# A convolution-mixer layer with a mixture of experts on one core: the gate's products on parts of the array, and other spacing of three stages

## The chip, the cores and the metric

The kernel runs on one core of one Trainium2 chip. The time is that of the device for one execution, in microseconds (us), from the first to the last instruction of the core; the number of a kernel is the median of its runs. Everything is in 32-bit floats. A core has these engines: PE (TensorE, matrix products; PEld is its loading of weights), DVE (VectorE), ACT (ScalarE, functions from tables and the eviction of PSUM), POOL (GpSimd), and SP, which here only issues DMAs. Each takes its instructions in the order in which the program has them.

## The reference, cut to what matters

For each of 4 images of 256 channels x 1024 positions:

```python
xs = x.reshape(B, C, N).transpose(0, 2, 1)            # after a norm over channels
xn = layernorm(xs, norm_w, norm_b)
xm = mamba_v(xc, ...) + skip_scale * xc               # 4 blocks of 64 channels, a selective scan over N
Q  = conv1d(conv1d(x_concat, qdw_w, qdw_b, groups=NB, pad=1), qpw_w, qpw_b)   # NB = 4 outputs, then 4x4
g  = sigmoid(Q);  xg = g * xm                         # one gate for each block of 64 channels
R  = conv1d(conv1d(xgt, rdw_w, rdw_b, groups=C, pad=1), rpw_w, rpw_b) + xgt
cat = concatenate([xs, R]);  xm2 = conv1d(conv1d(cat, fdw_w, fdw_b, groups=2*C, pad=1), fpw_w, fpw_b) + xs
x_local = conv1d(xm2, lc_w, lc_b, groups=C, pad=1);  x_global = mha(xm2, ...)  # 8 heads of 32
x_out = gelu(layernorm(concatenate([x_local, x_global]) @ fc_w.T + fc_b))
# norm over positions, 3x3 depthwise convolution, layernorm, product with proj_w, residual
# then for every position: norm, top 2 of 8 experts (256 -> 1024 -> gelu -> 256), weighted sum, residual
```

The change concerns `Q` and `g`, the end of the convolutions (`fpw_w`), the first norm of a next image, and the norms of the last image.

## The kernel before

The program is written in beats. In the main loop a beat is one step of the scan of the image at hand (32 states x 4 rows by 512 positions): the step's own instructions, and then one turn of each running generator, such as the convolutions of the image before. `yield n` in a generator means that it goes on n beats later. So the text decides where an instruction stands in its engine's queue; no scheduler moves it. Image b has 8 parts of 16 steps. The convolutions of image b-1 run in the first four parts of image b, its attention right after part 3, without scan steps beside it but the next ones. For the last image there is no scan left; its stages run beside tiles of the experts, each of 256 rows (64 products for a tile).

```python
def step(b, n, h, i):                                       # the scan
    dBu = ps(...)                                           # a PSUM tile
    nc.vector.tensor_tensor(dBu, dts[:, 1, :], bs, ALU.mult)
    nc.vector.tensor_tensor_scan(hs, dA, dBu, 0.0 if h == 0 else last, ALU.mult, ALU.add)
    if h == 0:
        nc.gpsimd.tensor_copy(last, hs[:, HALF - 1 : HALF])
    nc.gpsimd.tensor_tensor(hs, hs, cs, ALU.mult)
# bs: four products of PE on 32 columns each; dA: ACT; u: projection of the next block ("up", 4 products a half)

def in_turn(items, make, use, lag=2):
    made = []
    for at in range(len(items) + lag):
        if at >= lag:
            use(items[at - lag], made[at - lag])
        if at < len(items):
            made.append(make(items[at]))
        yield 1

def convolutions(b):
    ...                                                     # depthwise taps of xl, on ACT and DVE
    while not T.get(("whole", b)):
        yield 1
    xm = XM.pop(b)
    qs, qd = [], []
    for h in range(2):
        qd.append(ps(f"qd_{b}_{h}"))
        for i in range(6):
            c, k = divmod(i, 3)
            nc.tensor.matmul(qd[h][0:NB], qdwT_s[:, c, k, :], xm[:, c, ds(k + h * HALF, HALF)],
                             start=(i == 0), stop=(i == 5))
            if i % 3 == 2:
                yield 1
    for h in range(2):
        yield 1 - h
        qs.append(a2(f"qs_{b}_{h}", NB))
        nc.scalar.activation(qs[h], qd[h][0:NB], AF.Identity, bias=col("qdw_b", 0, slice(0, NB)))
    yield 1
    def gate(c): ...            # gp[h] = product of qpwT_s[:, ts(c, P)] (4 rows) and qs[h], both halves
    def sigmoid(c, gp): ...     # ACT, and back to the table of exp and ln
    yield from in_turn(range(NC2), gate, sigmoid)
    ...                         # POOL: xm = g * xm; taps of xm; rp = product with rpwT_s; residual on DVE; taps d4r
    yield from in_turn(CO_H, <fp: 4 products with fpwT_s into one PSUM tile>, mixed)   # mixed: DVE adds fp to xl
    yield from prepared(b)      # values (vp), queries and keys (qkp) of the attention

def normalised(b):              # first norm of an image to come
    ...
    for c in range(NC2):
        xl = a4(f"xl_{b}_{c}")
        nc.gpsimd.tensor_tensor(xl, xn[:, c, LEFT:], r1, ALU.mult)
        yield 1
        nc.vector.tensor_tensor(xn[:, c, LEFT:], xn[:, c, LEFT:], r2, ALU.mult)   # after POOL has read xn
        ...

def inverse_deviation(name, xc, alone):                     # alone: the last image
    ...
    for h in range(2):
        yield 1
        var.append(column_mean(f"var_{name}_{h}", sq[h]))
    for h in range(2):
        yield 1
        root(r[:, half(h)], var[h], eps5)                   # ACT: ln, then exp
    for c in range(NC2):
        nc.vector.tensor_tensor(xc[:, c, :], xc[:, c, :], r, ALU.mult)
        yield 1
```

Of the kernel before, what the change touches and what calls it, by code (L numbers as in the profile page):

```python
# [9 lines left out]
F32 = mybir.dt.float32  # L10
# [4 lines left out]
P = 128  # L15
# [57 lines left out]
def network(  # L73
# [70 lines left out]
    with tc.tile_pool(name="w_conv", bufs=1) as wp, tc.tile_pool(  # L144
# [33 lines left out]
        aoutT_s = load(aoutT, "aoutT_s")  # L178
        projT_s = load(projT, "projT_s")
        fcT_s = load(fcT, "fcT_s")  # L180
        qdwT_s = load(qdwT, "qdwT_s")
        qpwT_s = load(qpwT, "qpwT_s")
        rpwT_s = load(rpwT, "rpwT_s")
        fpwT_s = load(fpwT, "fpwT_s")
        wvT_s = load(wvT, "wvT_s")
# [9 lines left out]
        def later_weights():  # L195

            nc.sync.dma_start(vb, vbias.rearrange("a (c p) -> p (a c)", p=P))
            for t, ap in later:
                nc.sync.dma_start(t, ap)
                yield 1  # L200
            for ci in range(NC2):
                nc.sync.dma_start(
                    wqkT_s[:, ci].rearrange("p w (i x) -> p (w i) x", x=2 * HD)
                    .rearrange("p c (i x) -> p c i x", x=HD),
                    wqkT[:, ci].rearrange("p c (i x) -> p c i x", x=2 * HD)[:, :, :, 0:HD],
                )
                yield 1
            for i in range(4):
                at = _AT["qk_b"] + i // 2
                nc.sync.dma_start(  # L210
                    qk_b[ts(i, HD), :], vecs[ds(64 * (i % 2), HD), at : at + 8 : 2]
                )
                yield 1

            obp = ps_tile("obp")
            for co in range(NC2):
                for ci in range(NC2):
                    nc.tensor.matmul(
                        obp[:, co : co + 1], aoutT_s[:, ci, ts(co, P)], vb[:, ci : ci + 1],
                        start=(ci == 0), stop=(ci == NC2 - 1),  # L220
                    )
            yield 1
            nc.vector.tensor_tensor(
                ob, obp[:, 0:NC2], V[:, _AT["attn_outb"] : _AT["attn_outb"] + NC2], ALU.add
            )

            prp = ps_tile("prp")
            for co in range(NC2):
                for ci in range(NC2):
                    nc.tensor.matmul(  # L230
                        prp[:, co : co + 1], projT_s[:, ci, ts(co, P)], col("norm_b", ci),
                        start=(ci == 0), stop=(ci == NC2 - 1),
                    )
            yield 1
            nc.vector.tensor_tensor(
                prb, prp[:, 0:NC2], V[:, _AT["proj_b"] : _AT["proj_b"] + NC2], ALU.add
            )
            for ci in range(NC2):
                nc.vector.tensor_scalar(
                    projT_s[:, ci, :], projT_s[:, ci, :], col("norm_w", ci), None, ALU.mult  # L240
                )
            yield 1

            nc.vector.tensor_reduce(fcm, fcT_s, AX.X, ALU.add)
            yield 1
            nc.vector.tensor_scalar(fcm, fcm, 1.0 / C, None, ALU.mult)
            nc.vector.tensor_tensor(
                fcT_s, fcT_s, fcm.to_broadcast([P, 2 * NC2, C]), ALU.subtract
            )
            fbp = ps_tile("fbp")  # L250
            for c in range(NC2):
                nc.tensor.matmul(
                    fbp[:, 0:1], ones_mean, col("fc_b", c), start=(c == 0), stop=(c == NC2 - 1)
                )
            yield 1
            nc.vector.tensor_tensor(
                fcb, V[:, _AT["fc_b"] : _AT["fc_b"] + NC2], fbp[:, 0:1].to_broadcast([P, NC2]),
                ALU.subtract,
            )
# [113 lines left out]
                )  # L373
            return out

        def in_turn(items, make, use, lag=2):

            made = []
            for at in range(len(items) + lag):
                if at >= lag:  # L380
                    use(items[at - lag], made[at - lag])
                if at < len(items):
                    made.append(make(items[at]))
                yield 1

        CO_H = [(co, h) for co in range(NC2) for h in range(2)]

# [52 lines left out]
        def normalised(b):  # L440


            place_xn(b)
            xn = XN[b]

            def part(c, h):
                return xn[:, c, ds(LEFT + h * HALF, HALF)]

            yield 4

            def centre(h, mean):
                for c in range(NC2):
                    nc.vector.tensor_tensor(part(c, h), part(c, h), mean, ALU.subtract)

            yield from in_turn(
                range(2), lambda h: column_mean(f"mean_{b}_{h}", [part(c, h) for c in range(NC2)]),
                centre,
            )
            r1, r2 = a4(f"r1_{b}"), a4(f"r2_{b}")
            for h in range(2):  # L460
                sq = [a2(f"sq_{b}_{h}_{c}") for c in range(NC2)]
                for c in range(NC2):
                    nc.gpsimd.tensor_tensor(sq[c], part(c, h), part(c, h), ALU.mult)
                yield 1
                var = column_mean(f"var_{b}_{h}", sq)
                yield 2
                root(r1[:, half(h)], var, eps6)
                yield 1
                root(r2[:, half(h)], var, eps11, scale=1.0 + 1e-5)
                yield 1  # L470
            for c in range(NC2):
                xl = a4(f"xl_{b}_{c}")
                nc.gpsimd.tensor_tensor(xl, xn[:, c, LEFT:], r1, ALU.mult)
                yield 1
                nc.vector.tensor_tensor(xn[:, c, LEFT:], xn[:, c, LEFT:], r2, ALU.mult)
                yield 1
                nc.sync.dma_start(XL[b][:, c, :], xl)
                nc.gpsimd.tensor_scalar(
                    xn[:, c, LEFT:], xn[:, c, LEFT:], col("norm_w", c), col("norm_b", c),
                    ALU.mult, ALU.add,  # L480
                )
                yield 1
# [258 lines left out]
        def convolutions(b):  # L741
# [8 lines left out]
                yield 1  # L750
            xm = XM.pop(b)

            qs, qd = [], []
            for h in range(2):
                qd.append(ps(f"qd_{b}_{h}"))
                for i in range(6):
                    c, k = divmod(i, 3)
                    nc.tensor.matmul(
                        qd[h][0:NB], qdwT_s[:, c, k, :], xm[:, c, ds(k + h * HALF, HALF)],
                        start=(i == 0), stop=(i == 5),  # L760
                    )
                    if i % 3 == 2:
                        yield 1
            for h in range(2):
                yield 1 - h
                qs.append(a2(f"qs_{b}_{h}", NB))
                nc.scalar.activation(
                    qs[h], qd[h][0:NB], AF.Identity, bias=col("qdw_b", 0, slice(0, NB))
                )
            yield 1  # L770
            def gate(c):
                gp = []
                for h in range(2):
                    gp.append(ps(f"gp_{b}_{c}_{h}"))
                    nc.tensor.matmul(
                        gp[h], qpwT_s[:, ts(c, P)], qs[h], start=True, stop=True
                    )
                return gp

# [35 lines left out]
            def mixed(at, r):  # L815
# [5 lines left out]
                CO_H, lambda at: product(  # L821
                    f"fp_{b}_{at[0]}_{at[1]}", fpwT_s, at[0],
                    [d[ci // 2][:, ci % 2, half(at[1])] for ci in range(4)],
                ), mixed,
            )
            yield from prepared(b)

# [172 lines left out]
        def inverse_deviation(name, xc, alone):  # L1000

            r = a4(f"r_{name}")

            def squares(h):
                sq = [a2(f"sq_{name}_{h}_{c}") for c in range(NC2)]
                for c in range(NC2):
                    nc.scalar.activation(sq[c], xc[:, c, half(h)], AF.Square)
                return sq

            if alone:  # L1010
                sq = [squares(h) for h in range(2)]
                var = []
                for h in range(2):
                    yield 1
                    var.append(column_mean(f"var_{name}_{h}", sq[h]))
                for h in range(2):
                    yield 1
                    root(r[:, half(h)], var[h], eps5)
            else:
                for h in range(2):  # L1020
                    sq = squares(h)
                    yield 1
                    var = column_mean(f"var_{name}_{h}", sq)
                    yield 2
                    root(r[:, half(h)], var, eps5)
# [5 lines that stand above are left out]
# [998 lines left out]
```

## Time and profile before

| | |
|---|---|
| time, median of 3 runs | 2474.78 us (2465.03 to 2476.65) |
| span of the profiled execution | 2472.8 us |
| mean granted clock of PE | 0.906 of full |
| scan, first to last step | 60.6 to 1656.7 us |
| attention of images 0, 1, 2, 3 | from 510, 920, 1374, 1834 us |
| last rows of the last image sent to the experts | 2135.6 us |
| `qd` products (L758) | 96 records of 128x4 weights, 45.2 us busy, 592 ns each |
| `gp` products (L775) | 32 records of 4x128 weights, 17.3 us busy, 587 ns each |
| `qs` (L767) | 8 evictions of 4x512, 662 ns each |
| DVE's wait for POOL `xl` in the first norm (L475 for L473) | 7.3 us in 3 of 6 places |

How to read it: a product of 512 columns in 32-bit floats shows as two records in the trace. A share of busy time is an average over stages with different limits, so stretches of the span are looked at one by one: for each the busy time of every engine, the granted clock and the load of the DMA. In a line of the timeline stand the start, the time of one or more instructions in a row, engine, line and operation, output and inputs, shapes, the count, and in brackets the idle time before it with what ended it. A wait for several things is put down to the one that came last by the profile.

### The profile page before, as it was taken

To read this page: it belongs to the slowest core of one execution; us is meant where nothing else is said; L and a number is where in the kernel's file an instruction comes from. 1 tells how busy PE (TensorE), PEld (TensorE's weight loads), DVE (VectorE), ACT (ScalarE), POOL (GpSimd) and SP (SyncE) were. 2 spreads that over 40 slices of the span, in tenths; PEclk is the share of its full clock that TensorE was granted. 3 is DMA by queue.
4 is the path that set the end of the run, shared out by engine and by line. 5 is a ranking of instruction groups with operands and counts; after the bars stand their busy time and mean duration, and the time that the engine had idled before them with its cause. 6 is when DMAs were issued, how large, how long until landed. Compare 5 with 4: busy or idle time off the path is not lost. (4 is left out here: it accounts for less than half of the span.)

```text
span 2472.8 us, 28317 instructions
## 1 busy us (share of the span) xinstructions
PE 2134.3 (86%) x8810; PEld 947.7 (38%) x8810; DVE 1632.3 (66%) x2255; ACT 1194.4 (48%) x2019; POOL 1101.3 (45%) x1182
## 2 busy tenths in 40 slices
PE   7767768999977799987689999658999889899995
PEld 2111112322211132222123223114752568788885
DVE  3989898875898977789878787985525154211111
ACT  4554445468654548764254786325258533122221
POOL 0777776632676850366776205571130012322221
PEclk7888888899998899988788999768999989899997
DMA  3534433220334230043322202342340155766665
GB/s 90 138 99 111 99 95 78 60 56 27 74 94 108 72 76 26 22 115 91 112 74 57 48 18 59 88 154 88 90 124 1 45 152 162 211 197 193 193 197 157
DMA packets 154980, 244.30 MB, mean 99 GB/s; under 512 B 34184, under 2 KB 103452, under 8 KB 154816
## 3 DMA queue, kind: packets, MB, share of 16 engines
q1 hardware_dynamic: 135640, 217.05, 31.0%
q0 software_dynamic: 13264, 17.85, 3.7%
q10 hardware_dynamic: 5912, 7.45, 0.9%
q8 instruction: 74, 1.21, 0.2%
q14 instruction: 90, 0.74, 0.1%
HBM read 141.16 MB, written 33.98 MB: 71 GB/s over the span
## 5 line engine op out<-in xcount | busy, mean ns | idle before, releaser
L607 POOL TENSOR_TENSOR hs<-hs,cs 128x512 f32<-128x512 f32 x512 | 669.6, 1309 | 213.1 <-DVE hs L602 168.9
L613 PE MATMUL yp<-hs,quads 128*32 128x512 f32 x1024 | 342.3, 702 | 157.6 <-POOL hs L607 113.1
L588 ACT ACTIVATE dA<-dts,A 128x512 f32<-128x512 f32 x512 | 342.1, 713 | 276.3 <-DMA dts<-dt 194.4
L595 DVE TENSOR_TENSOR dBu<-dts,bs 128x512 f32<-128x512 f32 x512 | 347.8, 679 | 64.8 <-ACT u L517 13.3
L1896 POOL DMA_INDIRECT Y<-ys,dest x70 | 112.2, 1602 | 562.0 <-DVE ys L1890 555.5
L602 DVE TENSOR_TENSOR_SCAN hs<-dA,last,dBu 128x512 f32<-128x512 f32 x256 | 327.6, 1280 | 24.9 <-DVE dBu L595 0.5
L602 DVE TENSOR_TENSOR_SCAN hs<-dA,dBu 128x512 f32<-128x512 f32 x256 | 312.4, 1220 | 35.0 <-ACT dA L588 9.4
L928 ACT ACTIVATE e<-st 128x512 f32<-128x512 f32 x512 | 263.0, 606 | 90.0 <-PE st L918 89.1
L1875 ACT ACTIVATE hs<-h,b 128x256 f32<-128x256 f32 x280 | 116.8, 471 | 388.1 <-PE h L1870 233.0
L1880 PE MATMUL y<-w,hs 128*128 128x256 f32 x1120 | 266.1, 390 | 6.9 <-ACT hs L1875 6.9
L1870 PE MATMUL h<-xT,w 128*128 128x256 f32 x1120 | 252.4, 381 | 1.2 <-DVE xT L1848 1.2
L1848 DVE COPY xT<-xp 128x512 f32<-128x512 f32 x35 | 24.2, 691 | 323.5 <-PE xp L1847 308.5
L1880 PEld LDWEIGHTS y<-w,hs 128*128 128x128 f32 x1120 | 217.4, 197 | 46.2 <-issue 9.5
L606 POOL COPY last<-hs 128x1 f32<-128x1 f32 x256 | 66.5, 260 | 372.4 <-DVE hs L602 342.5
L1870 PEld LDWEIGHTS h<-xT,w 128*128 128x128 f32 x1120 | 213.2, 191 | 38.9 <-issue 8.4
L580 PE MATMUL bs<-u,xpwT_s 128*32 128x512 f32 x1024 | 184.9, 692 | 42.9 <-DVE hs L602 23.5
L613 PEld LDWEIGHTS yp<-hs,quads 128*32 128x32 f32 x1024 | 55.8, 120 | 409.5 <-POOL hs L607 271.1
L970 DVE TENSOR_TENSOR e<-e,e 128x512 f32<-128x512 f32 x256 | 171.3, 730 | 54.4 <-ACT e L928 27.6
L918 PE MATMUL st<-qk 32*128 32x512 f32 x1024 | 195.7, 658 | 7.9 <-DVE hs L602 4.5
L496 PE MATMUL up<-xn,inwk 64*128 64x512 f32 x256 | 140.5, 696 | 12.5 <-DVE hs L602 12.4
L960 PE MATMUL av<-e,v 128*32 128x512 f32 x1024 | 142.7, 625 | 0.0
L918 PEld LDWEIGHTS st<-qk 32*128 32x128 f32 x1024 | 68.4, 189 | 135.3 <-issue 89.2
(273 smaller groups left out, 2515.9 us busy)
## 6 DMA issues: line engine op xcount, KB each, us to landing
w<-in_W_dram SPq DMA_DIRECT2D x136, 512.0 KB
dts<-dt SPq DMA_DIRECT2D x512, 128.0 KB
cs<-cd SPq DMA_DIRECT2D x512, 64.0 KB
xs<-XS SPq DMA_DIRECT2D x35, 260.0 KB
b<-in_b_dram SPq DMA_DIRECT2D x35, 128.0 KB
xn<-in_x_dram SPq DMA_DIRECT2D x8, 512.0 KB
XL<-xl SPq DMA_DIRECT2D x8, 512.0 KB
xl<-XL SPq DMA_DIRECT2D x4, 1024.0 KB
```

Source lines behind the costliest of these rows:

```text
L580: nc.tensor.matmul(bs[r], xpwT_s[:, n, s : s + 1].to_broadcast([P, 32]), T[b, n, "u"][:, half(h)], start=True, stop=True,)
L588: nc.scalar.activation(dA, T[b, n, h, "dts", g][:, 0, :], AF.Exp, scale=A[:, g, n, q : q + 1])
L595: nc.vector.tensor_tensor(dBu, T[b, n, h, "dts", g][:, 1, :], T[b, n, h, "bs", q], ALU.mult)
L602: nc.vector.tensor_tensor_scan(hs, T[b, n, h, "dA", i], dBu, 0.0 if h == 0 else last, ALU.mult, ALU.add)
L607: nc.gpsimd.tensor_tensor(hs, hs, T[b, n, h, "cs", q], ALU.mult)
L613: nc.tensor.matmul(T[b, n, h, "yp"][ts(g, 32)], quads, T[b, n, h, "hs", q * GD + g], start=(q == 0), stop=(q == GS - 1),)
L918: nc.tensor.matmul(sts[i], k[r, ts(kt, P)], q[r, half(h)], start=True, stop=not shifted)
L928: nc.scalar.activation(es[i], sts[i], AF.Exp, scale=1.0 / HD**0.5)
L960: nc.tensor.matmul(accs[0][ts(i, HD)], v8[:, kt, ts(4 * g + i, HD)], es[i], start=(kt == 0), stop=(kt == NK - 1),)
L970: nc.vector.tensor_tensor(first[i], first[i], es[i], ALU.add)
L1870: nc.tensor.matmul(hp[:, i, :], w1(c, k), xT[:, c, :], start=(c == 0), stop=(c == NC2 - 1))
L1880: nc.tensor.matmul(yp[:, ts(t, C)], hs[:, k, ts(t, P)], w2(k), start=(k == 0), stop=(k == NHC - 1))
```

## The change

The `qd` products are split over four column groups of PE's array: group i makes half h and channel block c of one output tile, with h, c = divmod(i, 2), in three rounds for the three taps. Each takes 32 columns of the weights' tile, of which four are its own; the rest are later weights, whose results meet rows of zeros in the next product. That product sums the two channel blocks: its weights stand at rows 0, 32, 64 and 96 of a zeroed tile, and half h uses rows 64h to 64h + 63, one of two row groups. One eviction serves both halves, with the bias at rows 0 to 3 and 64 to 67. The weights' tiles are zeroed and loaded in the first image, over some more beats. The turns of `fp` take every second beat, with the same two beats from product to eviction, for all images but the last. In the first norm of a next image one more beat lies between POOL's and DVE's instruction. In the norms of the last image both roots come in one beat, and the product with them a beat later. The purpose is less time on PE for the gate, and fewer waits of engines for each other.

```diff
-        qdwT_s = load(qdwT, "qdwT_s")
-        qpwT_s = load(qpwT, "qpwT_s")
+        qdwT_s = wp.tile([P, NC2 * 3 * NB + 32 - NB], F32, name="qdwT_s")
+        qpwT_s = wp.tile([P, C], F32, name="qpwT_s")
+        qdw_b = wp.tile([P, 1], F32, name="qdw_b")
 ...        # later_weights()
+            for t in (qdwT_s, qpwT_s, qdw_b):
+                nc.gpsimd.memset(t, 0.0)
+            yield 1
+            nc.sync.dma_start(qdwT_s[:, 0 : NC2 * 3 * NB], qdwT.rearrange("p c k n -> p (c k n)"))
+            yield 1
+            for i in range(4):
+                nc.sync.dma_start(qpwT_s[32 * i : 32 * i + NB, :], qpwT)
+                if i % 2 == 0:
+                    at = _AT["qdw_b"]
+                    nc.sync.dma_start(qdw_b[32 * i : 32 * i + NB, :], vecs[0:NB, at : at + 1])
+                yield 1
 ...
-        def in_turn(items, make, use, lag=2):
-            made = []
+        def in_turn(items, make, use, lag=2, every=1):
+            made, lag = [], lag // every
 ...
-                yield 1
+                yield every
 ...        # normalised()
                 nc.gpsimd.tensor_tensor(xl, xn[:, c, LEFT:], r1, ALU.mult)
-                yield 1
+                yield 2
 ...        # convolutions()
-            qs, qd = [], []
-            for h in range(2):
-                qd.append(ps(f"qd_{b}_{h}"))
-                for i in range(6):
-                    c, k = divmod(i, 3)
+            qd, qs = ps(f"qd_{b}"), a2(f"qs_{b}")
+            for k in range(3):
+                for i in range(4):
+                    h, c = divmod(i, 2)
                     nc.tensor.matmul(
-                        qd[h][0:NB], qdwT_s[:, c, k, :], xm[:, c, ds(k + h * HALF, HALF)],
-                        start=(i == 0), stop=(i == 5),
+                        qd[ts(i, 32)], qdwT_s[:, ds((3 * c + k) * NB, 32)],
+                        xm[:, c, ds(k + h * HALF, HALF)],
+                        start=(k == 0), stop=(k == 2),
                     )
-                    if i % 3 == 2:
-                        yield 1
-            for h in range(2):
-                yield 1 - h
-                qs.append(a2(f"qs_{b}_{h}", NB))
-                nc.scalar.activation(
-                    qs[h], qd[h][0:NB], AF.Identity, bias=col("qdw_b", 0, slice(0, NB))
-                )
+                yield 1 if k else 0
+            yield 1
+            nc.scalar.activation(qs, qd, AF.Identity, bias=qdw_b)
 ...        # gate()
+                    r = ts(h, 64)
-                        gp[h], qpwT_s[:, ts(c, P)], qs[h], start=True, stop=True
+                        gp[h], qpwT_s[r, ts(c, P)], qs[r], start=True, stop=True
 ...
-                ), mixed,
+                ), mixed, every=1 if b == B - 1 else 2,
 ...        # inverse_deviation()
+                yield 1
                 for h in range(2):
-                    yield 1
                     root(r[:, half(h)], var[h], eps5)
+                yield 1
```

More of the change, by code (lines that the diff above doesn't have):

```diff
@@ L197, in later_weights @@
             nc.sync.dma_start(vb, vbias.rearrange("a (c p) -> p (a c)", p=P))
+            for t in (qdwT_s, qpwT_s, qdw_b):
+                nc.gpsimd.memset(t, 0.0)
+            yield 1
+            nc.sync.dma_start(
+                qdwT_s[:, 0 : NC2 * 3 * NB], qdwT.rearrange("p c k n -> p (c k n)")
+            )
+            yield 1
[5 more added lines that the diff above has]
+                yield 1
             for t, ap in later:
```

## The prediction

> **What bounds the kernel now.** I read the page first, then the busy time of each engine in stretches between milestones, then what each engine waited for, then the timeline at the spots where the engine that leads stood still. The chain that ended last covers only the final 2 us, so stretches carry the argument. From the page:
>
> ```profile
> PE 2134.3 (86%) x8810; PEld 947.7 (38%) x8810; DVE 1632.3 (66%) x2255; ACT 1194.4 (48%) x2019; POOL 1101.3 (45%) x1182
> ...
> PE   7767768999977799987689999658999889899995
> ...
> DVE  3989898875898977789878787985525154211111
> ```
>
> The reader is to see two regimes. Up to slice 27 (some 1660 us) DVE runs the scan and PE is full only in patches; from there PE is at 8 or 9 and DVE at 1 to 5. So in the first 1660 us PE time saved counts only where DVE, or a full PE, waits for it; after that it counts unless PE itself waits. Image 1's stretch that holds the convolutions of image 0 (us; then PE, PEld, DVE, ACT, POOL busy, clock, DMA share, GB/s):
>
> ```profile
> 344.10:387.50 43.40, 35.24 (x105) 8.95 (x106) 37.06 (x39) 22.36 (x32) 31.43 (x38) 0.88 0.41 110
> 387.50:431.70 44.20, 34.83 (x104) 8.93 (x104) 40.66 (x42) 23.91 (x34) 31.94 (x23) 0.81 0.28 66
> 431.70:482.00 50.30, 45.15 (x137) 17.21 (x138) 39.56 (x44) 20.64 (x30) 29.79 (x36) 0.86 0.26 61
> 482.00:510.30 28.30, 28.18 (x111) 9.61 (x109) 27.11 (x29) 18.36 (x31) 20.98 (x17) 1.00 0.32 79
> ```
>
> Each of the first three rows is a part of 16 scan steps. DVE idles 6.3, 3.5 and 10.7 us in them; the fourth row has PE without a gap, and the attention after it too. The idle DVE time has few causes; its timeline shows two in full:
>
> ```profile
> 386.73 0.70 DVE L595 TENSOR_TENSOR dBu<-dts,bs 128x512 f32<-128x512 f32 x1 [3.87 <-DMA cs<-cd]
> ...
> 467.55 0.75 DVE L818 SCALAR_TENSOR_TENSOR xl<-fp,V,xl 128x512 f32<-128x512 f32 x1 [4.51 <-PE fp L362]
> ...
> 474.81 0.75 DVE L818 SCALAR_TENSOR_TENSOR xl<-fp,V,xl 128x512 f32<-128x512 f32 x1 [4.65 <-PE fp L362]
> ```
>
> The first is put down to a DMA, but it ends 0.1 us after the last `bs` product, and PE's timeline shows `bs` standing behind the gate's products:
>
> ```profile
> 377.84 7.46 PE L758 MATMUL qd<-xm,qdwT_s 128*4 128x512 f32 x17
> 384.72 0.63 PE L580 MATMUL bs<-u,xpwT_s 128*32 128x512 f32 x3
> ```
>
> In images 2 and 3 the same wait is 3.87 and 3.86 us. I take it as PE's.
>
> **What the Trainium skill says.** (1) "TensorE: Matmul & The Clock Gate", Part 3 (packing small matmuls): products with different column groups, or different row groups, run concurrently, starts about 4 ns apart; four row groups measured 3.07x, three column groups 2.38x. The trace agrees for both kinds: the four `bs` products on 32 columns (L580) start within 0.02 us of one another, and so do the 32-row products of the logits (L918). (2) The same page, Part 1: an idle PE falls to half clock. The trace agrees: the same `bs` product takes 0.59 us at best and 1.06 us at worst, and the granted clock is 0.81 in the second row above. So a less busy PE may get some work back at half speed. (3) "TensorEngine Tiling (Array Packing)", Key Properties: a change of tiling mode drains PE. The trace has about 0.1 us for it (a product after a change starts 0.53 us later, not 0.43). (4) "ScalarE: Activation LUTs", What ACT_TABLE_LOAD costs: about 1283 ns; the trace has 1.28 us each.
>
> **The change, part by part.**
>
> *Gate's products.* A product of 512 columns is two records here, and in the timeline records of one group follow each 0.43 us, so 0.86 us a product. Before: 12 `qd` products in a row, 12 x 0.86 = 10.3 us an image. After: still 12, but three rounds of four column groups, 3 x 0.86 = 2.6 us. `gp`: four in a row, 3.4 us; after, two pairs on two row groups, 1.7 us. PE saves 7.7 + 1.7 = 9.4 us an image. ACT evicts once (128x512, some 0.68 us) instead of twice (0.66 each). In images 0 to 2 PE is not the bound there; what counts is DVE's waits: 3.87 goes, and of 0.83 (DVE waits for `u`, whose product stands between the `qd`) and 0.37 most. The 1.63 us behind the sigmoid stays, as it is ACT's table load. About 4.5 us x 3 images = 13.5 us.
>
> *Every second step.* The instruction order of both programs shows that PE's order from the first `fp` to the attention hardly changes; DVE gets one scan step (0.68 + 1.22 = 1.9 us) more between two `fp` evictions. The waits of 4.5 and 4.65 should fall to about 2 each. But PE has no gap between 449 and 510 us, so most of that only moves: DVE then waits for `bs` instead, or stands nearer to PE. What moves the end of this full stretch is work taken ahead of it: two `rp` outputs of two products each (4 x 0.86 = 3.4 us) go ahead, into a part with slack, and `op` and `zp` (1.7 us) fall behind the first `fp`. Net 1.7, I take 1.5 us x 3 = 4.5 us.
>
> *Wider spacing in the next norm.* DVE waited for the POOL product `xl` in 3 of 6 places, 7.3 us in all, in images 0 and 2 where DVE leads. One more scan step (1.9 us) lies between now. Waits above it keep a rest (3.09 - 1.9, 2.50 - 1.9). I take 5 us.
>
> *The last image (from 1656 us).* Here is no scan, and PE leads:
>
> ```profile
> 1656.00:1720.00 64.00, 52.19 (x141) 24.59 (x140) 39.36 (x50) 27.78 (x37) 13.75 (x12) 0.84 0.38 122
> 1720.00:1960.00 240.00, 238.52 (x1208) 128.34 (x1207) 92.68 (x196) 123.25 (x232) 32.86 (x48) 0.99 0.22 67
> 1960.00:2040.00 80.00, 63.21 (x250) 50.45 (x249) 38.96 (x75) 35.03 (x54) 14.47 (x12) 0.87 0.45 131
> ```
>
> 9.4 us of PE work go in the first row. But PE waits there already, 4.39 us at 1693 for DVE's 3x3 taps, which run without a gap from 1669 to 1693 and are not changed. With `qd` short, PE reaches that `mean` some 7 us sooner and waits longer for the same end. What stays is the gate's work that stood behind it (3.7 us, of which one pair of 0.9 remains) and part of the 2.57 us for `sq_fin`, as ACT gets the sigmoid earlier: I take 4 us. One expert tile (32 `h` and 32 `y` products, some 14 us) moves from ahead of the last attention to behind it, since the convolutions take fewer steps; PE is full to 2420 us either way, so this is even. In the third row the last norm's two roots now stand together: one pair of table loads less, 2 x 1.28 = 2.6 us of ACT, where PE waited 3.28 and 3.62 us for ACT's `hs`. I take 3 us.
>
> Sum: 13.5 + 4.5 + 5 + 4 + 3 = 30 us. Fixed costs (three memsets and five small weight loads more in image 0, where no view shows a wait for them) I take as nothing. As several terms hope that no other wait steps in, I take 28 us off 2474.8: 2447 us, 1.1% less.
>
> **Rivals.** *PE's saving counts in full:* 4 x 9.4 = 38 us, with 8 for norms and 4.5 for spacing some 50 us, 2425 us. For it: from the first `fp` to the end of the attention PE is full, and what precedes is 9.4 us shorter. Against it: in the first two rows DVE is busy 37 and 41 of 43 and 44 us, so at most 10 us can come out of both. *The wait only moves:* the in-order queues give a new wait wherever one falls. For it: the `mean` at 1693, PE's full stretch, and a clock that falls when PE idles more. Then only the three waits of 3.9 us and some of the norms count, 15 us, 2460 us. *The spreading hurts:* if values and query/key products, now pushed later, spilled over the end of part 3, the attention would start late, by 1.7 us for each query/key product left over (2 x 0.86). Against it: in the order of instructions the last query/key product still stands ahead of the last `yp` products, as before.
>
> **Range and chances.** The three times before spread over 12 us, so some 6 us of a difference is chance. The rivals give 2425 and 2460; eight in ten: 2427 to 2467 us. Faster by over 2% means below 2425.3, which needs the full saving: 0.09. Slower by over 2% needs a loss that no view points to: 0.01. Within 2%: 0.9.
>
> **What would show it.** `qd` should take 32 columns with four records starting together, and some 2.6 us an image instead of 10.3. DVE's wait of 3.87 before `dBu` in part 0 of images 1 to 3 should be gone and that part 38 to 39 us long instead of 43.4 and 43.5; the third part shorter by 2 to 4. DVE's waits for `xl` of POOL should sum to under 2.5 us. PE's wait for the taps before `mean` near 1690 should grow beyond 4.39; if it does not grow, the last image gains more than I say. One pair of table loads fewer in the last norm. I am wrong if DVE's wait returns elsewhere in part 0, if PE's clock falls below 0.81 there, or if the attention begins late.

## The result, and the profile after

| | before | after |
|---|---|---|
| median | 2471.09 us (4 runs, 2465.03 to 2476.65) | 2444.47 us (4 runs, 2442.67 to 2450.50) |
| ratio | | 0.9897 (95% interval 0.9864 to 0.9930) |
| once more, 11 and 6 runs | 2474.66 us | 2446.35 us, ratio 0.9885 (0.9862 to 0.9908) |
| profiled span, mean clock | 2472.8 us, 0.906 | 2441.0 us, 0.911 |
| scan ends | 1657.9 us | 1634.3 us |
| from there to the end | 814.9 us | 806.8 us |

The change is worth some 27 us, or 1.1%. The page of the kernel after, first its busy times and then PE's and DVE's slices:

```profile
PE 2086.5 (85%) x8810; PEld 933.9 (38%) x8810; DVE 1631.0 (67%) x2255; ACT 1189.7 (49%) x2013; POOL 1099.7 (45%) x1185
...
PE   7778767899977699987769999667999988899995
...
DVE  3888998875899988789988877986544253211111
```

PE has 47.8 us less to do with as many instructions. The two regimes are the same. The span fell by 31.8 us, less than PE's saving and more than the gate alone can explain. Where it fell shows in the same stretches of image 1 as before (columns as before):

```profile
345.60:384.40 38.80, 29.05 (x112) 8.15 (x112) 37.01 (x38) 21.04 (x30) 30.75 (x38) 0.87 0.40 110
384.40:430.40 46.00, 31.24 (x100) 6.69 (x96) 40.23 (x42) 26.17 (x36) 32.02 (x24) 0.82 0.29 76
430.40:476.90 46.50, 41.04 (x128) 14.62 (x128) 38.66 (x43) 20.79 (x32) 30.48 (x36) 0.92 0.27 68
```

Part 0 is 4.6 us shorter, part 1 is 1.8 us **longer**, part 2 is 3.8 us shorter. The next table counts all three images. Starts of the scan steps bound the parts, and the last column runs from part 3 to the end of the attention (us):

| | part 0 | part 1 | part 2 | part 3 and attention |
|---|---|---|---|---|
| before, images 1, 2, 3 | 43.4, 43.5, 52.3 | 44.2, 42.3, 44.4 | 50.3, 49.1, 50.1 | 129.8, 128.2, 125.0 |
| after, images 1, 2, 3 | 38.9, 38.7, 46.0 | 46.0, 45.8, 46.0 | 46.5, 46.5, 46.5 | 126.9, 126.6, 123.4 |
| gain, sum of three | 15.6 | -6.9 | 10.0 | 6.1 |

The gate (parts 0 and 1) gives 8.7 us and the end of the convolutions with the attention 16.1 us. A second profile of the changed kernel has 38.7, 40.2 and 48.5 us in part 0, so 11.8 us gained there and not 15.6, and 5.1 us for the gate. Most of the difference is one wait for ACT in part 0 of image 3, 4.34 us in the first profile and 7.45 us in the second; a wait of 7.34 us stood there before the change too. Image 0, which has no gate, is 2.0 us longer (285.5 for 283.5), and what follows the scan 8.1 us shorter. PE's timeline of part 0 of image 1 shows the products themselves:

```profile
373.04 1.89 PE L775 MATMUL qd<-xm,qdwT_s 128*32 128x512 f32 x16
374.86 3.70 PE L512 MATMUL up<-xn,inwk 64*128 64x512 f32 x8
378.49 1.06 PE L775 MATMUL qd<-xm,qdwT_s 128*32 128x512 f32 x8
379.37 1.04 PE L596 MATMUL bs<-u,xpwT_s 128*32 128x512 f32 x8
...
382.89 1.99 PE L789 MATMUL gp<-qs,qpwT_s 64*128 64x512 f32 x8 [1.62 <-ACT qs L782]
```

The 24 `qd` records take 2.95 us instead of some 10.6. `bs` stands right behind the last round. DVE's wait of 3.87 us before `dBu` in part 0 is gone in all three images. In its place stands one in part 1. DVE's timeline, line by line of one kernel:

```profile
398.71 2.27 DVE L411 SCALAR_TENSOR_TENSOR d<-xm,V,d 128x1024 f32<-128x1024 f32 x1 [2.73 <-ACT d L406]
...
464.32 0.75 DVE L832 SCALAR_TENSOR_TENSOR xl<-fp,V,xl 128x512 f32<-128x512 f32 x1 [3.84 <-PE fp L378]
471.58 0.75 DVE L832 SCALAR_TENSOR_TENSOR xl<-fp,V,xl 128x512 f32<-128x512 f32 x1 [2.74 <-PE fp L378]
```

The first is the first tap of the gated `xm`. The gate now needs two beats fewer, so the tap comes 10 scan steps after the gate's first product and not 12, and DVE reaches it before ACT, whose turn comes after its own sigmoids and POOL's product, has begun `d`. The other two are the waits of 4.51 and 4.65 us, shorter by 2.6 us together.

### The profile page after: what moved, and what is told of

Read it like the earlier page. It is cut to its first block, busy times and chain, and to the rows that moved or that the text cites. A ratio compares the mean times of both kernels' runs of the same rounds, so it can differ in the third digit from the quotient of the medians.

```text
span 2441.0 us, 28282 instructions
## 1 busy us (share of the span) xinstructions
PE 2086.5 (85%) x8810; PEld 933.9 (38%) x8810; DVE 1631.0 (67%) x2255; ACT 1189.7 (49%) x2013; POOL 1099.7 (45%) x1185
## 3 DMA queue, kind: packets, MB, share of 16 engines
q10 hardware_dynamic: 5912, 7.45, 0.9%
## 5 line engine op out<-in xcount | busy, mean ns | idle before, releaser
L984 DVE TENSOR_TENSOR e<-e,e 128x512 f32<-128x512 f32 x256 | 169.8, 725 | 64.1 <-PE av L974 31.6
L932 PE MATMUL st<-qk 32*128 32x512 f32 x1024 | 190.2, 649 | 3.5 <-ACT e L942 3.0
```

The costliest lines, as they stand in the source:

```text
L932: nc.tensor.matmul(sts[i], k[r, ts(kt, P)], q[r, half(h)], start=True, stop=not shifted)
L984: nc.vector.tensor_tensor(first[i], first[i], es[i], ALU.add)
```

## The experiments

All ratios are to the kernel before, run beside each one. Differences between variants are read from the parts of the scan; two profiles of the changed kernel agree within 0.3 us in eight of the twelve cells of the table above, and within 2.5 us in the others.

**One part, or all but one.** First the gate's products and their loads alone. The edit takes out the other three parts of the change:

```diff
-                ), mixed, every=1 if b == B - 1 else 2,
+                ), mixed,
...             # normalised()
-                yield 2
+                yield 1
...             # inverse_deviation(): the roots a beat apart, as before
```

> The kernel before plus the gate's products and their loads only; the end of the convolutions, the next norm and the last image's norms stand as before. Theory (short products and spacing add up): part 0 of images 1 to 3 keeps its gain, 38.7 to 39.5 us at first (before 43.5), the third part stays near 49 to 50 us, image 0 is about 4 us longer than before, as the norm's waits for POOL xl are back and the loads' shift stays; total 2452 to 2458 us. Rival (the gate's saving only moves to the next wait, and the spacing brings the gain): 2463 us or more, with part 1 longer by the same that part 0 is shorter.

Measured: 2466.72 us, ratio 0.9974 (0.9964 to 0.9984), so 6.4 us won. Part 0 is 39.3 and 38.7 us in images 1 and 2, as expected, and 47.9 us in image 3. But parts 1 and 3 lose: part 1 is 46.0 us (DVE waits 2.74 us for the tap there), part 3's scan steps take 34.4 us instead of 31.2, and part 3 with the attention 132.7, 131.7 and 129.4 us. Part 2 did not stay at 49 us but fell to 44.7 to 46.4, as, I take it, `fp` starts earlier and what it pushes away comes back in part 3. Over the three images part 0 wins 13.3 and part 2 12.0 us; part 1 loses 6.9, and part 3 with the attention 10.8. The total is the rival's.

Next, the PE time by itself. Beats, loads and everything else of the changed kernel, but the gate's products one after another:

```diff
-                        qd[ts(i, 32)], qdwT_s[:, ds((3 * c + k) * NB, 32)],
+                        qd[h][0:NB], qdwT_s[:, ds((3 * c + k) * NB, NB)],
...             # two evictions of 4 rows; gp from rows 0 to 3 only
```

> The changed kernel with the same beats, but the gate's 12 products one after the other into two tiles of 4 rows, two evictions, and the four second products on one row group: PE gets its 9.4 us an image back, and nothing else is undone. Theory (PE's time in front of bs makes DVE wait): part 0 is 43 us again in images 1 to 3 with a wait of about 3.9 us before dBu, and the total 2455 to 2460 us. Rival (the shorter span of beats, not PE's time, made the gain): part 0 stays below 40 us and the total is within 4 us of the changed kernel's 2444.5. In the last image PE's wait for the taps before the mean should fall from 10.5 to some 4 us with little change of the tail: below 5 us.

Measured: 2466.58 us, ratio 0.9970 (0.9957 to 0.9983). Part 0 is 48.9, 48.4 and 54.9 us, so longer than before the change, and the stretch after the scan 810.7 us for 806.8. DVE waits for what stands behind the gate's products. Its one long wait in part 0, and PE's queue ahead of it:

```profile
395.32 0.70 DVE L611 TENSOR_TENSOR dBu<-dts,bs 128x512 f32<-128x512 f32 x1 [9.54 <-ACT qs L784]
```

```profile
379.54 7.85 PE L775 MATMUL qd<-xm,qdwT_s 128*4 128x512 f32 x16
387.32 3.70 PE L512 MATMUL up<-xn,inwk 64*128 64x512 f32 x8
390.95 3.17 PE L775 MATMUL qd<-xm,qdwT_s 128*4 128x512 f32 x7
393.53 0.63 PE L596 MATMUL bs<-u,xpwT_s 128*32 128x512 f32 x3
```

The line names ACT's `qs`, which evicts the gate's products and ends 0.03 us before; the last `bs` record ends within 0.1 us of the same moment. The trace doesn't part the two, but both stand behind the 12 serial products. The wait is 9.54 us and not 3.9 because 16 of the 24 `qd` records, and not 6 as in the kernel before, now stand ahead of `up`, which `bs` needs too (through `u`): the closer beats are harmful without the short products. The short products are worth some 20 us here, in beats that suit them. In the last image PE's wait before `mean` is 3.86 us instead of 10.47, as expected, and the attention starts 157.5 us after the scan's end instead of 153.1.

Then `fp` back in every beat, the rest as changed:

```diff
-                ), mixed, every=1 if b == B - 1 else 2,
+                ), mixed,
```

> The changed kernel with the fp products back in every beat in all images. Theory of the prediction: DVE's waits for fp in the third part go back from 3.8 and 2.7 to near 4.5 and 4.6 us, but PE is full there, so only 1.5 us an image are lost: 2447 to 2451 us in all, with the third part about 1.5 us longer. Rival (spacing in the third part is worth as much as its row of lengths suggests, 2.6 to 3.8 us an image): 2453 us or more. Second rival (nothing, as PE is full): 2443 to 2446 us.

Measured: 2462.53 us, ratio 0.9959 (0.9942 to 0.9975): undoing this one part loses 15 to 18 us of the 27, against 4.5 predicted. My own sum is beaten by the rival, and by more than the rival said. The place is part 3 and the attention (132.8, 131.8, 128.3 us against 126.9, 126.6, 123.4); part 2 hardly differs. Part 3's scan steps of image 2 in both kernels, first with `fp` in every beat, then the changed kernel:

```profile
885.88:920.26 34.38, 32.32 (x122) 11.76 (x122) 29.99 (x32) 21.07 (x35) 22.94 (x19) 1.00 0.31 77
```

```profile
879.90:910.95 31.05, 30.91 (x125) 11.98 (x123) 29.68 (x33) 17.25 (x29) 22.86 (x19) 1.00 0.32 79
```

DVE idles 4.4 us in the first and 1.4 us in the second. `every=2` spreads `fp` alone; the values and the queries and keys (`qkp`) still take a beat each, but start four beats later. With `fp` in every beat `qkp` come earlier, eight records in a row ahead of the scan's products. DVE's waits and PE's queue around them:

```profile
899.36 0.70 DVE L611 TENSOR_TENSOR dBu<-dts,bs 128x512 f32<-128x512 f32 x1 [0.87 <-ACT qk L907]
905.13 0.76 DVE L650 SCALAR_TENSOR_TENSOR xm<-xn,V,op 64x512 f32<-64x512 f32 x1 [1.65 <-PE op L644]
```

```profile
896.62 3.70 PE L378 MATMUL qkp<-xl,wqkT_s 128*128 128x512 f32 x8
900.25 1.06 PE L596 MATMUL bs<-u,xpwT_s 128*32 128x512 f32 x8
...
915.09 1.04 PE L629 MATMUL yp<-hs,quads 128*32 128x512 f32 x2 [0.79 <-POOL hs L623]
916.07 1.13 PE L932 MATMUL st<-qk 32*128 32x512 f32 x6
917.63 1.12 PE L932 MATMUL st<-qk 32*128 32x512 f32 x2 [0.43 <-DVE hs L618]
919.59 1.34 PE L932 MATMUL st<-qk 32*128 32x512 f32 x3 [0.84 <-DVE hs L618]
```

DVE's first wait ends with ACT's eviction of a `qkp` tile (`dBu` takes its PSUM tile from the same pool), the second with `op`, which stands behind `qkp`. So DVE falls behind while `qkp` hold the queue. Then PE has run out of `qkp` and waits at the end of part 3 and at the first logits (`st`) for the last scan steps. These waits at `st` don't come from the steps' delay: the kernel before has them too (0.45, 0.87 and 0.20 us), with part 3's steps at 31.2 us. In the changed kernel the last `qkp` run while DVE does the last steps, and `st` follow without a gap on PE:

```profile
909.55 3.85 PE L932 MATMUL st<-qk 32*128 32x512 f32 x16
```

From the first of these 16 records to the product behind them it is 3.8 us in images 0 to 2, and 6.7 to 7.5 us in every kernel with `fp` in every beat, the one before included. The wait of DVE for the last `yp` at the start of the attention, 5.71 us with `fp` in every beat (5.84 before the change) and 3.18 us in the changed kernel, carries this on. No run parts the wider spacing of `fp` from the later place of what follows it.

Last of these four, POOL's and DVE's instruction of the next norm close together again:

```diff
-                yield 2
+                yield 1
```

> The changed kernel with POOL's and DVE's instruction of the next norm one beat apart again. Theory of the prediction: 5 us lost, 2449 to 2450 us. From the lengths of the parts: only image 0 gained (3 us in its fourth part) and image 2 only changed the name of its waits, so 2446 to 2449 us, with image 2's parts 4 and 5 still 46 and 42 us. Rival (the spacing is worth nothing or costs): 2444 us or less.

Measured: 2445.77 us, ratio 0.9899 (0.9877 to 0.9921), which can't be told from the changed kernel. The mechanism is there, in image 0, on DVE's timeline:

```profile
177.57 2.27 DVE L491 TENSOR_TENSOR xn<-xn,r 128x1024 f32<-128x1024 f32 x1 [1.34 <-POOL xl L489]
189.46 2.27 DVE L491 TENSOR_TENSOR xn<-xn,r 128x1024 f32<-128x1024 f32 x1 [3.10 <-POOL xl L489]
```

The changed kernel has one such wait, of 2.51 us, and its fourth part of image 0 is 39.1 us for 42.2. In image 2 the parts are 46.3 and 42.5 us in both kernels: there the wait only changed its name.

**Which of the two, the beats of before or `every=2`?** The gate alone had lost in parts 1 and 3 most of what it won in parts 0 and 2. On that kernel, two beats more between the gated `xm` and its taps put all that follows back to the beats of before:

```diff
+            yield 2
             for c in range(NC2):
                 yield from depthwise3(d[1], c, xm, c, "rdw_w", c, col("rdw_b", c))
```

> The gate alone (fp in every beat, norms as before) plus two beats between the gated xm and its taps, so that all that follows stands at the same beats as in the kernel before. Alone without them the gate gave 7 us only, with part 3 and the attention 132.7, 131.7 and 129.4 us long (129.8, 128.2, 125.0 before). Theory (the shorter gate brought the values and query/key products two beats ahead, where they stand before bs, and every=2 only repairs that): part 3's scan steps take 31.2 us again instead of 34.4, part 3 and attention 125 to 130 us, part 0 stays below 40 us, total 2452 to 2458 us. Rival (spacing of fp itself, not the place of what follows): part 3 stays at 34 us and the total at 2463 us or more.

Measured: 2453.51 us, ratio 0.9942 (0.9920 to 0.9963), so 14.3 us won and not 6.4. The expected total came, but not all for the expected reason. Part 3's steps do take 31.2 us again; yet part 2 grows to 50.6, 49.9 and 47.7 us, with the old wait for `fp` back (4.40 us), so from part 2 to the end of the attention it is 180.1, 178.0 and 172.9 us against 177.4, 178.0 and 175.8: nothing won in the sum. The gain is part 1, 42.6 us instead of 46.0 in each image. So the gate's haste costs at the tap, and from `fp` on it is `every=2` that counts, by the spacing or by the four later beats: with it that stretch is 173.4, 173.1 and 169.9 us in the changed kernel.

The same edit on the changed kernel:

> The changed kernel with two more beats between the gated xm and its taps. DVE's wait of 2.73 us for ACT's first tap in part 1 should fall below 1 us, and part 1 be 43 us instead of 46 in images 1 to 3: 2438 to 2441 us, if the values and query/key products, then two beats later, still end in part 3. Rival (they spill over and the attention begins late): part 3's scan steps and the attention together 129 us or more instead of 126.6, total 2446 us or more.

Measured: 2428.89 us, ratio 0.9843 (0.9823 to 0.9864). Part 1 is 42.6, 42.4 and 42.6 us, the wait for the tap 0.19 us, and the stretch from part 2 to the attention's end is not longer (173.4, 173.4, 166.5). Nothing spilled over. The total is better than I expected. The three parts 1 account for 10.2 us, and image 3's last stretch for 3.4 more, which stays unexplained; by the ratios the edit is worth 10 to 13 us, by the medians 16.

**The image that has no gate.** The gate's loads last among the weights:

```diff
-            for t in (qdwT_s, qpwT_s, qdw_b): ...      # memsets and loads ahead of the other weights
+            yield 2
...             # and the same memsets and loads after fcb, the last work on weights
```

> The changed kernel with the gate's memsets and loads after all other weights' work, so that this work stands at the beats of the kernel before. If the four beats that the loads push it later cost the 5.8 us that image 0's first two parts grew by, part 1 of image 0 is 36 us instead of 41 and the total 2439 to 2441 us. Rival (the clock's low stretch moved there by chance, as image 0 varies by 8 us between profiles of the same work): within 2 us of 2444.5 us.

Measured: 2432.84 us, ratio 0.9844 (0.9828 to 0.9860). Part 1 of image 0 is 35.5 us, before the change 35.5 as well, and 41.4 in the changed kernel. In ten profiles with the early loads it is 39.9 to 42.3 us, in three with the late ones 35.5. So the loads' place costs 5.9 us: it moved the one-time work on other weights (`projT`, `fcT`, `fcb`) four beats on, from the end of part 0 and the start of part 1 well into part 1. That part with the late loads, and then in the changed kernel:

```profile
91.60:127.10 35.50, 23.39 (x76) 4.41 (x76) 33.73 (x39) 14.15 (x23) 25.09 (x24) 0.90 0.45 111
```

```profile
91.70:133.10 41.40, 27.72 (x93) 7.00 (x92) 36.59 (x43) 14.74 (x23) 24.34 (x22) 0.84 0.41 101
```

DVE has 2.9 us more to do there and idles 3.0 us more; part 0 did not get shorter for it (31.6 us in both). The rest of the 12 us is not explained: in this profile the stretch after the scan is 799.6 us for 806.8, with the same instructions.

**ACT behind the tap's wait.** The gate's four sigmoids in one beat, one pair of table loads instead of two, POOL's product one beat earlier and the taps where they were:

```diff
-            yield from in_turn(range(NC2), gate, sigmoid)     # sigmoid(c) ends with the table of exp and ln
+            # gate(0), a beat, gate(1), a beat, then both sigmoids, then log_exp() once, a beat
...
-                yield 1                                        # after each of POOL's products
+                yield 1 + c
```

> The changed kernel with the gate's four sigmoids in one beat behind one table load, and the taps at the same beat as before: 2.56 us of table loads fewer on ACT for each image. If part 1's waits (1.57 us behind the sigmoids, 2.73 us for ACT's first tap) come from ACT's two pairs of table loads, the second falls below 0.5 us, the first grows to some 2.8 us at most, and part 1 is 1.5 to 3 us shorter in images 1 to 3: 2437 to 2441 us. Rival (POOL's product or PE behind it sets that wait): no change of part 1 beyond 1 us, 2443 to 2446 us.

Measured: 2425.15 us, ratio 0.9825 (0.9804 to 0.9847). Part 1 is 42.7, 42.8 and 43.0 us, 3.1 us shorter. The tap's wait is gone, and the wait behind the sigmoids did not grow (1.45 us). Part 1 of image 1, to be held against the row of 46.00 us above:

```profile
379.64:422.34 42.70, 28.72 (x98) 6.61 (x96) 39.79 (x43) 23.36 (x34) 31.99 (x24) 0.92 0.33 81
```

ACT is 2.8 us less busy. As POOL's product also stands a beat earlier here, table loads and beat together removed the wait; this run doesn't part them. The total fell by more than the 9.3 us that the three parts show; the rest is not explained.

**The changed kernel again, the roots, and combinations.** The changed kernel once more:

> The changed kernel once more, as the base of the runs beside it: 2441 to 2450 us, ratio 0.986 to 0.993, part 3's scan steps 31.0 to 31.4 us in images 1 to 3. If it comes out below 2436 us, what the single edits won over 2444.5 us has to be read as less.

Measured: 2446.35 us, ratio 0.9885 (0.9862 to 0.9908), as expected. The roots of the last image's norms apart again:

```diff
-                yield 1
                 for h in range(2):
+                    yield 1
                     root(r[:, half(h)], var[h], eps5)
-                yield 1
```

> The changed kernel with the roots of the last image's norms in two beats again, with the beat of the product as before. Prediction's term: 3 us lost for a pair of table loads, all after the last scan step; total 2446 to 2449 us with that stretch 809 to 811 us instead of 807, and a wait of PE for the expert's hs of over 6 us in the last norm (0.6 and 4.4 now, 3.3 and 3.6 before). Rival (PE's queue fills it): within 1 us.

Measured: 2447.02 us, ratio 0.9899 (0.9877 to 0.9921), within the noise of the changed kernel. Its stretch after the scan is 810.7 us for 806.8 and 807.1, and PE's waits are back:

```profile
1930.17 1.13 PE L1894 MATMUL y<-w,hs 128*128 128x256 f32 x4 [3.28 <-ACT hs L1889]
1935.86 2.08 PE L1894 MATMUL y<-w,hs 128*128 128x256 f32 x4 [4.56 <-ACT hs L1889]
```

In the changed kernel one long wait is left (and one of 0.57 us):

```profile
1934.13 2.07 PE L1895 MATMUL y<-w,hs 128*128 128x256 f32 x4 [4.43 <-ACT hs L1890]
```

The stretch after the scan can't size this: it is 799.6 us in `loads_late` and 810.5 in `fp_every_beat`, whose edits leave that stretch as in the changed kernel. A shorter piece can: from the last logits to the last `mean` it is 107.4 to 109.6 us in the ten profiles with the roots together, 112.2 to 112.6 in the four with them apart. So the roots are worth 3 to 5 us there; the medians are too coarse to confirm it.

Sigmoids together and late loads in one kernel:

> The changed kernel with the four sigmoids in one beat and the gate's loads after the other weights. Alone the first gave 2425 and the second 2433 us. If both are real and independent: part 1 of image 0 at 35.5 us and part 1 of images 1 to 3 at 42.7 to 43 us together, 2412 to 2420 us. If each was partly chance of the clock: 2424 to 2432 us.

Measured: 2429.11 us, ratio 0.9814 (0.9792 to 0.9837). Part 1 has both gains (35.5 us in image 0; 42.8, 43.1 and 42.8 us), but the total is not the 2412 to 2420 us of two independent gains and can't be told from that of the sigmoids alone. Part 2 of image 0 took 48.0 us in its profile, 38.5 to 39.5 us in most others; more on this at the end.

With four beats ahead of the mean of image 2's last norm as well:

```diff
             nc.sync.dma_start(xr, x[b].rearrange("(c p) n -> p c n", p=P))
+            if b == B - 2:
+                yield 4
```

> The same as best, with four beats between the last tap and the mean in the last norm of image 2, so that the second pair of the gate's products, eight products y and four xp stand ahead of the mean in PE's queue, where PE waited 10.5 us for DVE's taps. If that wait is where the gate's saving of the last image went, it falls to 4 to 6 us and the total is 4 to 6 us below best. Rival (the norm's chain then sets the end of that stretch): within 2 us of best or above it.

Measured: 2433.44 us, ratio 0.9842 (0.9821 to 0.9864), not better than without it. The gate's second pair and `y` do stand ahead of the mean now, and PE still waits 10.95 us for the taps (10.47 without). The stretch after the scan is 810.8 us. The rival's side, then; what sets that stretch's length, other than the taps themselves, stays open.

## Why the prediction was right, and where its steps were not

The total, 2447 us, came close to 2444.5, and in part by luck: the list of steps did not fit, and errors of opposite sign met.

| step | predicted gain | measured |
|---|---|---|
| gate in images 0 to 2 | 13.5 us | part 0: 15.6 (11.8 in a second profile); part 1: -6.9 (-6.7); so 5 to 9 |
| every second step | 4.5 us | 16.1 in the parts; 15 to 18 when undone |
| wider spacing in the next norm | 5 us | 3.1 in image 0, 0 in image 2; not separable in the total |
| last image: gate and roots | 4 + 3 us | 4.4 (gate, to the start of the attention) + 3 to 5 (roots); 8.1 in all, with up to 11 us of chance |
| loads and memsets | 0 | -5.9 in image 0's part 1 |

*Gate's products.* The products' times were right (2.95 us measured for 2.6), and so was the reading that the 3.87 us wait "put down to a DMA" was PE's: it is gone with the short products and 9.54 us with serial ones in closer beats. Part 0 came out at 38.9 and 38.7 us in images 1 and 2, in the range of 38 to 39 that I gave (46.0 in image 3, which started from 52.3). The clock there was 0.87, 0.79 and 0.78, so in two images below the 0.81 that I had named as a sign of being wrong; image 2's part was short all the same. What failed is that I counted the waits that go and looked for a new one in part 0 only. I had seen that the gate takes fewer beats and used it for the experts' tiles alone. The two beats also brought DVE to the tap too early: it waits 2.73 us in each image.

*Every second step.* The step that failed is "PE has no gap between 449 and 510 us, so most of that only moves". It is drawn from one kernel's picture, and a PE that shows no gap is not one that can give nothing. In image 1, from part 2 to the end of the attention, PE was busy 173.4 us before with 880 records and 167.5 us after with 881: a PE that is busy 96% of a stretch still had 5.9 us in it. In images 2 and 3 its busy time fell by 2.1 and 1.7 us only, and its idle time by 2.1 and 3.6. In image 1 the granted clock rose in the same stretch (0.86 to 0.92 in part 2, 0.97 to 1.00 in the attention); in image 2 part 2 has 0.93 both times and is still 2.6 us shorter. How much is the clock and how much the order was not parted. The net of 1.5 us an image was a count of work moved across a boundary; it left out that the attention's first products wait for the last scan steps, and that later `qkp` fill that time.

*Norm.* Summing 7.3 us of waits took each wait as removable time. In image 2 DVE met the next wait at once. The sum of waits for POOL fell to 2.51 us, about as I said, and yet the parts there kept their lengths: that sign came true for a step that was only half right.

*Last image.* Right in mechanism, and in size as far as the shorter pieces show it. PE waits 10.47 us before the mean instead of 4.39, for the same taps; before and after:

```profile
1693.39 5.46 PE L371 MATMUL mean<-xi,ones_mean 128*128 128x512 f32 x6 [4.39 <-DVE xi L1108]
```

```profile
1672.08 2.08 PE L387 MATMUL mean<-xi,ones_mean 128*128 128x512 f32 x2 [10.47 <-DVE xi L1123]
```

So 6.1 us of what the gate saves in the last image (9.4 by the prediction) went into this wait. With the products serial again it is 3.86 us.

*Loads.* "No view shows a wait for them" was true and beside the point: the loads cost nothing themselves, but they stand in a generator whose later turns carry DVE and PE work.

Of the rivals, "PE's saving counts in full" is out, as the gate alone won 6.4 us; "the wait only moves" was true in part, of the norm, the last image and part 1; "the spreading hurts" did not come true in any run, and with `taps_later` even two beats more left the attention on time.

## What to carry to other kernels

When a stage in an in-order beat schedule gets shorter, find what stands behind it, and give back the beats that its consumers needed: here two empty beats won 10 us in the scan's parts, against some 27 us for the whole change. An engine that a trace shows as busy throughout may still finish sooner when its work stands in another order; try the order on the chip instead of ruling it out. And check what one-time work moves when something is put ahead of it in the same generator.

## What the runs showed of the hardware that I had not expected

Four column groups brought 24 records from some 10.6 to 2.95 us (3.6 times), two row groups brought eight `gp` records from 3.69 us (in the serial run) to 1.99 us (1.85 times); four and two times would be the ideal. All are products of 512 columns in 32-bit floats.

One stretch of image 0, its third part, which no edit but the place of the loads touches, took 38.5 to 48.0 us from profile to profile, and the granted clock goes with it: 0.87 to 0.91 in the ten profiles of 38.5 to 39.5 us, 0.77 at 43.7 and 44.7 us, 0.65 and 0.68 at 48.0 and 47.6 us. The changed kernel and then the serial one, busy times in that stretch:

```profile
133.00:172.00 39.00, 30.94 (x104) 9.34 (x104) 32.72 (x38) 20.85 (x32) 30.14 (x41) 0.87 0.42 113
```

```profile
133.00:181.00 48.00, 39.77 (x97) 11.92 (x97) 33.16 (x40) 20.87 (x31) 30.58 (x41) 0.68 0.36 96
```

DVE works 33 us in both; PE takes 8.8 us more for no more records, and DVE waits once for 7.2 us for `bs`. Two profiles of the changed kernel itself have 39.1 and 44.7 us, so no edit is needed for the low clock to fall there, and its effect is large enough to hide any part of this change worth less than some 5 us in the medians.
